# A two-layer graph kernel: batch 0's norm factor put on the adjacency, its halves in two PSUM banks, the mask's operations issued singly, and the second group's second pair normed in the result tiles

## The chip, the core and the metric

The kernel runs on one core of a Trainium2 chip. Five engines work side by side, each through its own list of instructions in order: TensorE (PE, matrix products into PSUM), VectorE (DVE), ScalarE (ACT), GpSimd (POOL) and SyncE (SP, which here issues every DMA). PSUM has eight banks of 128 x 512 float32, named b0 to b7 below. The metric is the device time in microseconds; lower is better.

## What is computed

128 graphs ("batches") of 128 nodes with 512 features, one adjacency for all. Cut to what matters:

```python
def _layernorm(x, axis=-1, eps=1e-5):
    m = jnp.mean(x, axis=axis, keepdims=True)
    v = jnp.var(x, axis=axis, keepdims=True)
    return (x - m) / jnp.sqrt(v + eps)

# layer 0
h = jnp.maximum(_layernorm(x), 0.0)
y = jnp.einsum('nm,bmd->bnd', adj, h)
x = x + jnp.einsum('bnd,do->bno', y, weight) + bias
# layer 1: 8 heads of 64; attn_mask is adj
h = jnp.maximum(_layernorm(x), 0.0)
q, k, v = split(h @ w_qkv)
attn = softmax(where(adj == 0, -inf, q @ k.T * scale))
o = (attn @ v) @ w_proj + b_proj
x = x + o + _layernorm(o) * ln_gamma + ln_beta
```

## The kernel before

The program first collects operations in a list, then a planner orders them, and only then are they issued. `Plan.op` (line 68) takes the engine, an assumed duration, the buffers read and written, and either a due time (`due`) or, for PE, a place (`at`). `schedule` (line 102) walks through time and gives each free engine the ready operation with the smallest due; `early` forbids a start before that time, `urgent` keeps the engine free for an operation that is about to be ready. A buffer is a name out of a group (the table `G`, line 255): it takes a slot such as t20 when its first operation is placed and gives it back after its last. So a changed due or slot can move instructions far from the edit. The planner's times are assumptions of the program; what the chip runs is the resulting order on each engine, with semaphores between them.

**First phase (layer 0).** `phase1` (line 481), one batch at a time for batches 0 to 3, in pairs afterwards. A batch's x is loaded (`load`, line 308); `stats` gives mean and 1/sigma (on DVE for batches 0 to 5: bn_stats and bn_aggr on L393 and L394, then `ve`, POOL's `pow`, and `shift` = -mean/sigma on L404); ACT writes h0 = relu(x/sigma + shift) (L491); four PE matmuls (`mix`, L499) make y = (adj h0) transposed in one PSUM bank, with the transposed adjacency `adjT`; y is copied out. For batches 0 to 3 four float32 matmuls (L508) multiply y with the raw weight tiles `raw0`, which lie in f0 to f3. Later batches split y into three parts (L445 to L447) and do twelve faster fp32r matmuls (L457) against `wA`, the weight split in the same way by `split_weights` (L353 to L357). DVE adds the product to x (L510, or L465 and L470), and the sum is stored twice, as x1d and, with beta added, as x1b.

**The filler.** PE starts with 5 matmuls of the identity on itself (L323), transposes the adjacency (L326), and does 12 more (L332, three operations of four). Their results are not used.

**The mask.** `mask_ops` (line 337) makes from the adjacency an additive mask `maskb`, in six DVE instructions (L339 to L344) that are one operation of the plan, assumed at 1.4, not before 60.

**Second phase (layer 1).** 32 groups of four batches, `phase2_group` (line 571). `fetch` (line 539) brings a pair: x1d is loaded into `xn` (t20, t21), normed with ACT (L555) into `hx` (t22, t23, two slots for all pairs), sent through DRAM and back for a block transpose, transposed on DVE (L559), and split into three parts `hp` by ACT (L562, L565) and POOL (L563, L566). `hp` holds six batches, so batches 6 and 7 write where 0 and 1 were. A group then does q and k (L594, 96 matmuls), the attention products of the group before (L721), scores (L649), v and the projection of the group before (both L457). The second pair of a group is due 8 before the group's start `t0`, 12 for the group with j = 1:

```python
        for p in range(2):
            fetch(group[2 * p:2 * p + 2], t0 - (37, 8 if j != 1 else 12)[p])
```

Slots t18 and t19 are the group "o", in which the projection's results are summed and normed (`sum_up`, L465 and L468). The first of them are written while the second group is computed.

The last groups end with unsplit products and their own norm; no edit touches them.

Of the kernel before, what the change touches and what calls it, by code (L numbers as in the profile page):

```python
# [11 lines left out]
AF = mybir.ActivationFunctionType  # L12
# [3 lines left out]
P = 128  # L16
# [197 lines left out]
def kernel(  # L214
# [77 lines left out]
    def time1(i):  # L292
        return START1 + 4.3 * min(i, FIRST) + T1 * max(i - FIRST, 0)
# [31 lines left out]
    op("PE", 2.2, lambda: idle(5), r=[ident], w=[pa], at=-20)  # L325
# [8 lines left out]
    for _ in range(3):  # L334
        op("PE", 0.9, lambda: idle2(4), r=[ident], w=[pb], at=0)

    def mask_ops():
        e = adj_sb.ap[:, :P]
        nc.vector.tensor_scalar(e, e, 0.0, None, op0=ALU.not_equal)  # L339
        nc.vector.tensor_reduce(some.ap[:, :1], e, AX.X, ALU.max)  # L340
        nc.vector.reciprocal(some.ap[:, :1], some.ap[:, :1])
        nc.vector.tensor_scalar(some.ap[:, :1], some.ap[:, :1], 0.0, None, op0=ALU.mult)
        nc.vector.tensor_scalar(e, e, 1.0, MASKED, op0=ALU.subtract, op1=ALU.mult)
        nc.vector.tensor_scalar(maskb.ap, e, some.ap[:, :1], None, op0=ALU.add)  # L344

    op("DVE", 1.4, mask_ops, r=[adj_sb], w=[adj_sb, some, maskb], due=100, early=60)
# [134 lines left out]
    def phase1(batches):  # L481
        for i in batches:
            if i not in X:
# [3 lines left out]
                       early=6.2 if batches == [1] else 0.0)  # L487
        for n, i in enumerate(batches):
# [12 lines left out]
            if i < FIRST:  # L501
                y = buf("y", [P, C, P])
                op("ACT", 0.53, lambda y=y, p=p: nc.scalar.copy(y.ap, p.ap), r=[p], w=[y], what="y")
# [16 lines left out]
            dma(lambda i=i: X1B[i].ap, lambda i=i: X[i].ap, 256, due=ti + 12, r=[X[i]], w=[X1B[i]], what="x1b out")  # L520

# [17 lines left out]
    def fetch(pair, due):  # L539
# [31 lines left out]
    def phase2_group(j):  # L571
        group = tuple(range(4 * j, 4 * j + 4))
        t0 = START2 + T4 * j
# [5 lines left out]
        for p in range(2):  # L579
            fetch(group[2 * p:2 * p + 2], t0 - (37, 8 if j != 1 else 12)[p])  # L580
# [43 lines left out]
        for n, i in enumerate(group):  # L624
# [3 lines left out]
            op("ACT", 0.53, lambda v=v, a=a: nc.scalar.activation(v.ap, a.ap, AF.Copy, scale=UP), r=[a], w=[v], due=tv + 1, what="vA")  # L628
# [132 lines left out]
    for i in range(FIRST):  # L761
        phase1([i])
# [56 lines left out]
```

## Time and profile before

| | us |
|---|---|
| runs (three) | 2130.49, 2132.52, 2132.86 |
| median | 2132.52 |
| the profiled execution, its own time | 2131.4 |
| its span, first to last instruction | 2129.6 |
| PE busy within the span | 2114.8 |
| first phase's first product with `wA` (L457) begins | 27.79 |
| q and k of the first group (L594) begin | 478.2 |
| q and k of the second group begin | 517.49 |
| PE's last matmul ends | 2121.6 |

The profile gives the instructions of one execution by engine. "PE b L457" is a matmul of line 457 into a PSUM bank; a float32 matmul stands in it as two records, an fp32r matmul as one, so the counts of L323, L332, L499 and L508 are twice the instructions. Where an engine idled, the profile names the instruction that ended the wait. Lines are those of the program before; the edits move them by some tens in the program after.

### The profile page before, as it was taken

The numbers are of one execution on the slowest core, as the hardware profiler recorded it, in microseconds if no ns is written. First come the engines' busy times: TensorE is split into PE (matmuls) and PEld (weight loads), VectorE is DVE, ScalarE is ACT, GpSimd is POOL, SyncE is SP. The second block draws the span as 40 slices with busy tenths as digits, with TensorE's granted clock in tenths as the row PEclk, the third lists the DMA queues.
The fourth block names the chain that finished last, engine by engine and source line by source line (L and its number), as shares of the span: only waits on it lengthen the run. The fifth ranks groups of instructions, "written<-read, shape, count | busy, mean of one in ns | idle before, by whom it ended". The sixth has DMA issues, their size and how long they took to land.

```text
span 2129.6 us, 44884 instructions
## 1 busy us (share of the span) xinstructions
PE 2114.8 (99%) x14867; PEld 1778.1 (83%) x14867; DVE 1729.3 (81%) x3275; ACT 1478.5 (69%) x4240; POOL 1524.9 (72%) x1280
## 2 busy tenths in 40 slices
PE   9999999999999999999999999999999999999998
PEld 7888888887888888888888888888888888888885
DVE  7889888877788778888888887877777788887877
ACT  7777777777666666666666666666666666666664
POOL 6888878794567777776667777777777767677765
PEclk9999999999999999999999999999999999999999
DMA  6676666674655565565556655666666666655553
GB/s 229 222 238 233 229 223 215 232 238 159 189 191 182 182 184 183 180 188 179 179 179 185 195 189 185 190 193 190 186 188 187 188 187 194 192 183 183 182 164 120
DMA packets 297880, 410.96 MB, mean 193 GB/s; under 512 B 33072, under 2 KB 163248, under 8 KB 297648
## 3 DMA queue, kind: packets, MB, share of 16 engines
q1 hardware_dynamic: 297648, 408.09, 60.7%
q8 instruction: 118, 1.93, 0.4%
q14 instruction: 114, 0.93, 0.1%
HBM read 207.68 MB, written 200.28 MB: 192 GB/s over the span
## 4 chain that ended last, share of the span: by engine, by line
PE 94%; DVE 2%; DMA 2%; ACT 1%; issue 1%; SPq 0%; POOL 0%; DVEq 0%; ACTq 0%
PE b L457 47%; PE b L594 32%; PE b L721 5%; PE b L649 5%; PE b L499 5%; DMA t<-in_x_dram 1%; DVE f L659 0%; ACT f L671 0%; DMA f<-in_L_gnn_weight_dram 0%; DMA f<-in_x_dram 0%; DMA d<-t 0%; DVE t L755 0%; DVE wA L357 0%; DVE t L753 0%; DVE t L446 0%
## 5 line engine op out<-in xcount | busy, mean ns | idle before, releaser
L457 PE MATMUL b<-wA,t 128*128 128x512 f32 x2976 | 727.4, 393 | 0.8 <-DVE t L447 0.8
L594 PE MATMUL b<-hp,wqk 128*128 128x512 f32 x3072 | 701.6, 389 | 2.6 <-ACT hp L562 2.6
L594 PEld LDWEIGHTS b<-hp,wqk 128*128 128x128 f32 x3072 | 576.6, 188 | 122.6 <-ACT hp L562 3.0
L457 PEld LDWEIGHTS b<-wA,t 128*128 128x128 f32 x2976 | 549.6, 188 | 109.8 <-DVE t L447 1.2
L671 ACT ACTIVATE f<-f,n 128x128 f32<-128x128 f32 x1024 | 395.8, 389 | 1.3
L747 POOL TENSOR_TENSOR t<-t,t 128x512 f32<-128x512 f32 x128 | 165.9, 1296 | 317.3 <-DVE t L468 247.1
L457 PE MATMUL b<-wv,hp 128*128 128x512 f32 x1536 | 373.0, 392 | 0.6 <-DVE f L659 0.6
L457 PEld LDWEIGHTS b<-wv,hp 128*128 128x128 f32 x1536 | 285.9, 188 | 64.6 <-DVE f L659 6.0
L677 POOL TENSOR_TENSOR f<-f,n 128x1024 f32<-128x1024 f32 x126 | 242.1, 1921 | 65.8 <-PE b L457 42.9
L601 ACT ACTIVATE t<-b 128x512 f32<-128x512 f32 x256 | 148.2, 592 | 199.7 <-PE b L594 199.6
L702 DVE STREAM_TRANSPOSE f<-f 128x1024 f32<-128x1024 f32 x126 | 156.3, 1241 | 130.3 <-DMA f<-d 126.7
L602 DVE TENSOR_TENSOR t<-b,t 128x512 f32<-128x512 f32 x256 | 173.8, 690 | 83.3 <-PE b L594 74.9
L445 ACT ACTIVATE t<-b 128x512 fp32r<-128x512 f32 x248 | 146.6, 592 | 85.0 <-PE b L499 39.8
L446 DVE TENSOR_TENSOR t<-b,t 128x512 fp32r<-128x512 f32 x248 | 170.4, 687 | 38.4 <-ACT t L445 37.0
L671 ACT ACTIVATION_READ_ACCUMULATOR f<-f,n 128x1 f32 x1024 | 193.3, 189 | 0.0
L750 POOL TENSOR_TENSOR t<-t,gamma_b 128x512 f32<-128x512 f32 x122 | 157.7, 1293 | 38.3 <-ACT t L749 38.3
L563 POOL TENSOR_TENSOR hp<-t,hp 128x512 fp32r<-128x512 f32 x128 | 164.6, 1293 | 25.2 <-DMA t<-x1b 14.1
L447 DVE SCALAR_TENSOR_TENSOR t<-t,b 128x512 fp32r<-128x512 f32 x248 | 168.4, 679 | 8.2
L659 DVE TENSOR_TENSOR f<-b,maskb 128x512 f32<-128x512 f32 x256 | 156.6, 682 | 17.4 <-PE b L649 17.4
L566 POOL TENSOR_TENSOR hp<-hp 128x512 fp32r<-128x512 f32 x128 | 165.1, 1300 | 0.2
L555 ACT ACTIVATE t<-t,m 128x512 f32<-128x512 f32 x128 | 97.1, 807 | 91.7 <-DVE m L435 91.7
L751 POOL TENSOR_TENSOR t<-t,t 128x512 f32<-128x512 f32 x122 | 157.4, 1290 | 2.5
(122 smaller groups left out, 3159.8 us busy)
## 6 DMA issues: line engine op xcount, KB each, us to landing
d<-f SPq DMA_DIRECT2D x126, 512.0 KB, 3.5
f<-d SPq DMA_DIRECT2D x504, 128.0 KB, 3.8
t<-x1d SPq DMA_DIRECT2D x128, 256.0 KB, 4.0
d<-t SPq DMA_DIRECT2D x128, 256.0 KB, 4.0
t<-d SPq DMA_DIRECT2D x512, 64.0 KB, 2.3
t<-x1b SPq DMA_DIRECT2D x128, 256.0 KB, 3.0
out_dram<-t SPq DMA_DIRECT2D x128, 256.0 KB, 3.2
t<-in_x_dram SPq DMA_DIRECT2D x91, 256.0 KB, 3.0
```

Source lines behind the costliest of these rows:

```text
L446: op("DVE", 0.63, lambda: nc.vector.tensor_tensor(l.ap, p.ap, h.ap.bitcast(F32), op=ALU.subtract), r=[p, h], w=[l], what=name + "l", due=d ...
L447: op("DVE", 0.63, lambda: nc.vector.scalar_tensor_tensor(s.ap, h.ap.bitcast(F32), UP, p.ap, op0=ALU.mult, op1=ALU.subtract), r=[p, h], w=[ ...
L457: nc.tensor.matmul(p.ap, lhsT=parts[m][2]()[:, c], rhs=w.ap[:, m, c, :], start=start and c == 0, stop=stop and c == C - 1)
L563: op("POOL", 1.35, lambda ht=ht, h=h, l=l: nc.gpsimd.tensor_tensor(l(), ht(), h().bitcast(F32), op=ALU.subtract), r=[h1, HP[i, 0]], w=[HP[ ...
L566: op("POOL", 1.38, lambda l=l, s=s: nc.gpsimd.tensor_tensor(s(), s().bitcast(F32), l().bitcast(F32), op=ALU.subtract), r=[HP[i, 1]], w=[HP ...
L594: nc.tensor.matmul(p.ap, lhsT=wqk.ap[:, which, c, col:col + P], rhs=hp[:, pick, :, which, c, :], start=start and c == 0, stop=stop and c = ...
L602: op("DVE", 0.63, lambda r=r, b=b: nc.vector.tensor_tensor(r.ap, b.ap, r.ap, op=ALU.add), r=[b], w=[r], due=tg + (4 if g < 7 else 2), what ...
L671: nc.scalar.activation(v[:, h], v[:, h], AF.Exp, bias=mx.ap[:, h:h + 1], scale=scale, accum_out=mx.ap[:, H + h:H + h + 1])
L677: op("POOL", 1.93, lambda heads=heads, mx=mx: nc.gpsimd.tensor_tensor(heads().rearrange("p h q r -> p q h r"), heads().rearrange("p h q r ...
L747: op("POOL", 1.32, lambda x1=x1, o=o: nc.gpsimd.tensor_tensor(x1.ap, x1.ap, o.ap, op=ALU.add), r=[o], w=[x1], due=tl + (3 if rank > 1 else ...
L750: op("POOL", 1.32, lambda o=o: nc.gpsimd.tensor_tensor(o.ap, o.ap, gamma_b.ap, op=ALU.mult), r=[gamma_b], w=[o], due=tl + 7, what="gamma")
L751: op("POOL", 1.32, lambda x1=x1, o=o: nc.gpsimd.tensor_tensor(o.ap, o.ap, x1.ap, op=ALU.add), r=[x1], w=[o], due=tl + 9, what="out")
```

## The change

Five edits.

1. Batch 0 gets its own function, `first_batch`. Its x is loaded in two halves of 256 columns, ahead of the adjacency. Each half has its own bn_stats. DVE, no longer ACT, writes h0 = max(x - mean, 0), without the factor 1/sigma; since that factor is positive and belongs to a row of h0, it can stand on the rows of the transposed adjacency, which DVE scales into `adjS` in a free part of the adjacency's tile. Mix, copy and product are done in halves, the two halves of mix in two PSUM banks.
2. The filler is 6 matmuls before the transposition and 3 after it, for 5 and 12.
3. For batches 1 to 3 the product with the raw weight is two operations of two matmuls; the copy of y is urgent. Batch 1's statistics may start at 4.8, for 6.2.
4. The six mask instructions are operations of their own, with starts not before 60, 75, 90, 105, 120 and 135.
5. In the second phase, batches 6 and 7 use the slots of "o" (t18, t19) as `hx`. The second pair is due 20, 20 and 11 before `t0` for the first three groups; all groups but the first have a `t0` smaller by 3; the first group's v copy is due 5 sooner.

```diff
-    load(0, -9)
+    X[0] = buf("x", [P, D])
     adj_sb = buf("raw", [P, D])
-    dma(lambda: adj_sb.ap[:, :P], lambda: adj, 64, due=-8.5, w=[adj_sb], what="adj")
+    dma(lambda: X[0].ap[:, :D // 2], lambda: x[0][:, :D // 2], 128, w=[(X[0], 0)], what="load", due=-60)
+    dma(lambda: X[0].ap[:, D // 2:], lambda: x[0][:, D // 2:], 128, w=[(X[0], 1)], what="load", due=-59)
+    dma(lambda: adj_sb.ap[:, :P], lambda: adj, 64, due=-58, w=[adj_sb], what="adj")
...
-    op("PE", 2.2, lambda: idle(5), r=[ident], w=[pa], at=-20)
+    op("PE", 2.75, lambda: idle(6), r=[ident], w=[pa], at=-20)
...
-    for _ in range(3):
-        op("PE", 0.9, lambda: idle2(4), r=[ident], w=[pb], at=0)
...
-    op("DVE", 1.4, mask_ops, r=[adj_sb], w=[adj_sb, some, maskb], due=100, early=60)
+    op("PE", 1.4, lambda: idle2(3), r=[ident, pa], w=[pb], at=0)
...
-                       early=6.2 if batches == [1] else 0.0)
+                       early=4.8 if batches == [1] else 0.0)
...
-                def plain(a=a, y=y):
-                    for c in range(C):
-                        nc.tensor.matmul(a.ap, lhsT=y.ap[:, c], rhs=raw0[c].ap, start=c == 0, stop=c == C - 1)
-                op("PE", 3.43, plain, r=[y] + raw0, w=[a], at=ti, what="l0")
+                for k in range(2):
+                    def plain(k=k, a=a, y=y):
+                        for c in (2 * k, 2 * k + 1):
+                            nc.tensor.matmul(a.ap, lhsT=y.ap[:, c], rhs=raw0[c].ap, start=c == 0, stop=c == C - 1)
+                    op("PE", 1.72, plain, r=[y] + raw0[2 * k:2 * k + 2], w=[a], at=ti + 0.1 * k, what="l0")
...
+    def first_batch():
+
+        half = lambda b, k: b.ap[:, k * (D // 2):(k + 1) * (D // 2)]
+        h0, t, ends = buf("h0", [P, D]), buf("st1", [P, 16]), buf("st1", [P, 16])
+        for k in range(2):
+            op("DVE", 0.42, lambda k=k: nc.vector.bn_stats(ends.ap[:, 6 * k:6 * k + 6], half(X[0], k)), r=[(X[0], k)], w=[(ends, k)], what="bn")
+        op("DVE", 0.2, lambda: nc.vector.bn_aggr(t.ap[:, 12:14], ends.ap[:, :12]), r=[ends], w=[(t, 0)], what="bn")
+        op("DVE", 0.17, lambda: nc.vector.tensor_scalar(t.ap[:, 6:7], t.ap[:, 13:14], EPS, None, op0=ALU.add), r=[(t, 0)], w=[(t, "ve")], what="ve")
+        op("POOL", 0.71, lambda: nc.gpsimd.tensor_tensor(t.ap[:, 8:9], t.ap[:, 6:7], minus_half.ap[:, :1], op=ALU.pow), r=[(t, "ve"), minus_half], w=[(t, "rs")], what="pow")
+        adjS = View(adj_sb, lambda ap: ap[:, P:2 * P])
+        op("DVE", 0.45, lambda: nc.vector.tensor_scalar(h0.ap, X[0].ap, t.ap[:, 12:13], 0.0, op0=ALU.subtract, op1=ALU.max), r=[X[0], (t, 0)], w=[h0], due=-20, what="relu0")
+        op("DVE", 0.2, lambda: nc.vector.tensor_scalar(adjS(), adjT.ap, t.ap[:, 8:9], None, op0=ALU.mult), r=[adjT, (t, "rs")], w=[(adj_sb, "s")], due=-20, what="adjS")
+        p, y, a = [buf("ps", [P, 2, P]) for _ in range(2)], buf("y", [P, C, P]), buf("ps", [P, D])
+        for k in range(2):
+            def mix(k=k):
+                for c in (2 * k, 2 * k + 1):
+                    nc.tensor.matmul(p[k].ap[:, c - 2 * k, :], lhsT=h0.ap[:, c * P:(c + 1) * P], rhs=adjS(), start=True, stop=True)
+            MIX[0] = op("PE", 0.45, mix, r=[h0, (adj_sb, "s")], w=[p[k]], at=-10 + k, what="mix")
+            op("ACT", 0.35, lambda k=k: nc.scalar.copy(y.ap[:, 2 * k:2 * k + 2, :], p[k].ap), r=[p[k]], w=[(y, k)], due=-18 + k, what="y", urgent=True)
...
+            op("PE", 1.72, plain, r=[(y, k)] + raw0[2 * k:2 * k + 2], w=[a], at=time1(0) + 0.1 * k, what="l0")
...
-            HX.append(buf("hx", [P, Q, C, R]))
+            HX.append(buf("o" if 6 <= i < 8 else "hx", [P, Q, C, R]))
...
-        t0 = START2 + T4 * j
+        t0 = START2 + T4 * j - (3.0 if j else 0.0)
...
-            fetch(group[2 * p:2 * p + 2], t0 - (37, 8 if j != 1 else 12)[p])
+            fetch(group[2 * p:2 * p + 2], t0 - (37, (20, 20, 11)[j] if j < 3 else 8)[p])
...
+        (0.26, lambda: nc.vector.tensor_scalar(edges(), edges(), 0.0, None, op0=ALU.not_equal)),
+        (0.29, lambda: nc.vector.tensor_reduce(one(), edges(), AX.X, ALU.max)),
+        (0.16, lambda: nc.vector.reciprocal(one(), one())),
+        (0.15, lambda: nc.vector.tensor_scalar(one(), one(), 0.0, None, op0=ALU.mult)),
+        (0.8, lambda: nc.vector.tensor_scalar(edges(), edges(), 1.0, MASKED, op0=ALU.subtract, op1=ALU.mult)),
+        (1.2, lambda: nc.vector.tensor_scalar(maskb.ap, edges(), one(), None, op0=ALU.add)),
+    )):
+        op("DVE", us, f, r=[adj_sb], w=[adj_sb, some, maskb], due=300, early=60 + 15.0 * k, what="edges")
```

The times in the code are the planner's assumptions, not measurements.

More of the change, by code (lines that the diff above doesn't have):

```diff
@@ L332, in idle2 @@
             nc.tensor.matmul(pb.ap, lhsT=ident.ap, rhs=ident.ap, start=True, stop=True)
-    for _ in range(3):
-        op("PE", 0.9, lambda: idle2(4), r=[ident], w=[pb], at=0)
[L337 to L344, printed above, removed]
-    op("DVE", 1.4, mask_ops, r=[adj_sb], w=[adj_sb, some, maskb], due=100, early=60)
+    op("PE", 1.4, lambda: idle2(3), r=[ident, pa], w=[pb], at=0)
     def split_weights(w, c, col, raw, low, due, gap, early=0.0):
@@ L502, in phase1 @@
                 y = buf("y", [P, C, P])
-                op("ACT", 0.53, lambda y=y, p=p: nc.scalar.copy(y.ap, p.ap), r=[p], w=[y], what="y")
+                op("ACT", 0.53, lambda y=y, p=p: nc.scalar.copy(y.ap, p.ap), r=[p], w=[y], what="y", urgent=True)
                 a = buf("ps", [P, D])
-                def plain(a=a, y=y):
-                    for c in range(C):
-                        nc.tensor.matmul(a.ap, lhsT=y.ap[:, c], rhs=raw0[c].ap, start=c == 0, stop=c == C - 1)
-                op("PE", 3.43, plain, r=[y] + raw0, w=[a], at=ti, what="l0")
+                for k in range(2):
[3 more added lines that the diff above has]
+                    op("PE", 1.72, plain, r=[y] + raw0[2 * k:2 * k + 2], w=[a], at=ti + 0.1 * k, what="l0")
                 op("DVE", 0.68, lambda i=i, a=a: nc.vector.scalar_tensor_tensor(X[i].ap, a.ap, 1.0, X[i].ap, op0=ALU.mult, op1=ALU.add, accum_out=mean(i)),
@@ L520, in phase1, with plain @@
             dma(lambda i=i: X1B[i].ap, lambda i=i: X[i].ap, 256, due=ti + 12, r=[X[i]], w=[X1B[i]], what="x1b out")
+    def first_batch():
[16 more added lines that the diff above has]
+            op("ACT", 0.35, lambda k=k: nc.scalar.copy(y.ap[:, 2 * k:2 * k + 2, :], p[k].ap), r=[p[k]], w=[(y, k)], due=-18 + k, what="y", urgent=True)
+            def plain(k=k):
+                for c in (2 * k, 2 * k + 1):
+                    nc.tensor.matmul(a.ap, lhsT=y.ap[:, c], rhs=raw0[c].ap, start=c == 0, stop=c == C - 1)
+            op("PE", 1.72, plain, r=[(y, k)] + raw0[2 * k:2 * k + 2], w=[a], at=time1(0) + 0.1 * k, what="l0")
+        op("POOL", 1.32, lambda: nc.gpsimd.tensor_tensor(X[0].ap, X[0].ap, b0_b.ap, op=ALU.add), r=[b0_b], w=[X[0]], due=time1(0) + 1, what="b0")
+        finish1(0, a)
@@ new lines, in finish1 @@
+    def finish1(i, a):
+        ti = time1(i)
+        op("DVE", 0.68, lambda: nc.vector.scalar_tensor_tensor(X[i].ap, a.ap, 1.0, X[i].ap, op0=ALU.mult, op1=ALU.add, accum_out=mean(i)),
+           r=[a], w=[X[i], (means, i)], due=ti + 5, what="x1")
+        X1D[i] = in_dram([P, D], "x1d")
+        dma(lambda: X1D[i].ap, lambda: X[i].ap, 256, due=ti + 6, r=[X[i]], w=[X1D[i]], what="x1 out")
+        X1B[i] = in_dram([P, D], "x1b")
+        op("POOL", 1.32, lambda: nc.gpsimd.tensor_tensor(X[i].ap, X[i].ap, beta_b.ap, op=ALU.add), r=[beta_b], w=[X[i]], due=ti + 10, what="beta")
+        dma(lambda: X1B[i].ap, lambda: X[i].ap, 256, due=ti + 12, r=[X[i]], w=[X1B[i]], what="x1b out")
@@ L627, in phase2_group @@
             a, b = times_weights([(HP[i, m], None, part(i, m)) for m in range(3)], wv, tv, "v", [v])
-            op("ACT", 0.53, lambda v=v, a=a: nc.scalar.activation(v.ap, a.ap, AF.Copy, scale=UP), r=[a], w=[v], due=tv + 1, what="vA")
+            op("ACT", 0.53, lambda v=v, a=a: nc.scalar.activation(v.ap, a.ap, AF.Copy, scale=UP), r=[a], w=[v], due=tv + (1 if j else -4), what="vA")
             op("DVE", 0.63, lambda v=v, b=b: nc.vector.tensor_tensor(v.ap, b.ap, v.ap, op=ALU.add), r=[b], w=[v], due=tv + 2, what="vB")
@@ L759, in rest_of @@
         return PT, finish
-    for i in range(FIRST):
+    first_batch()
+    edges = View(adj_sb, lambda ap: ap[:, :P])
+    one = lambda: some.ap[:, :1]
+    for k, (us, f) in enumerate((
+        (0.26, lambda: nc.vector.tensor_scalar(edges(), edges(), 0.0, None, op0=ALU.not_equal)),
[6 more added lines that the diff above has]
+        op("DVE", us, f, r=[adj_sb], w=[adj_sb, some, maskb], due=300, early=60 + 15.0 * k, what="edges")
+    for i in range(1, FIRST):
         phase1([i])
```

## The prediction

> **What bounds the kernel now.** I read the page's busy shares, then who kept TensorE (PE) waiting in the whole span, then the chain of waits of the first 60 us, then rows around each wait. From the page:
>
> ```profile
> PE 2114.8 (99%) x14867; PEld 1778.1 (83%) x14867; DVE 1729.3 (81%) x3275; ACT 1478.5 (69%) x4240; POOL 1524.9 (72%) x1280
> ```
>
> PE is the bound from end to end; only time in which it idles or does filler can be won. The list of its waits (total, times, longest, us) is short:
>
> ```profile
> PE b L594 <- ACT hp L562: 2.6, 1, 2.6
> PE b L323 <- POOL t masks.py:199: 1.4, 1, 1.4
> PE b L499 <- ACT t L491: 1.0, 2, 0.6
> PE b L457 <- DVE t L447: 0.8, 1, 0.8
> PE b L457 <- DVE f L659: 0.6, 1, 0.6
> PE b L649 <- DVE t L447: 0.4, 1, 0.4
> ```
>
> In the timeline they stand at 514.9 (2.57), 0 (1.36), 13.5 (0.40) and 38.0 (0.58), 67.4 (0.81), 2079.3 (0.63) and 545.3 (0.38). Two more stretches carry no work: the filler matmuls (L323, L332), up to 8.07, and the tail after PE's last matmul, 2121.6 to 2129.6. The instruction lists of the two programs are the same on every engine from the third group's first products on (some 590 us), so the tail and the 0.63 stay. What is at stake: the first 28 us, 0.58, 0.81, 2.57 and 0.38.
>
> **The start.** The chain of waits (start, length, what), pieces left out:
>
> ```profile
> 2.11 5.37 DMA f<-in_L_gnn_weight_dram
> 7.50 6.86 DMA t<-in_x_dram
> ...
> 14.38 0.71 DVE m L393
> ...
> 26.16 1.08 DVE wA L357
> ```
>
> It does not pass through batch 0's norm, mix or product. SP's twelfth DMA (x of batch 4) is issued only when the first weight tile has landed (7.48), lands at 14.36, and then VectorE (DVE) is busy without a break: statistics of batches 4 and 5, the splitting of the weight (L354, L357), updates L510. The split weight wA is whole at 27.23, and
>
> ```profile
> 27.79 3.01 PE L457 MATMUL b<-wA,t 128*128 128x512 f32 x12
> ```
>
> is the first product that needs it, of three-part products it does for the rest of the phase.
>
> *The front half.* By rows: x0 landed at 4.06; as two 128 KB DMAs issued at 0.74 and 1.18 I put it at 3.6 (estimate). Two half statistics (0.69 for a whole, so some 0.4 each), 0.18, then max(x-m,0) on DVE (not in the trace; between 0.33, half of L447's 0.67 for such a tile, and ACT's 0.81 that it replaces; I take 0.5), then, by the list, batch 1's statistics (0.87), which wait for x1 (landing 5.0), then the scaled adjacency (128x128: L339's 0.22). That is ready at 6.2. POOL's pow (0.56) lies beside; the two half copies on ACT (0.59 for a whole, between 0.27 and 0.4 each) end before the weights land. Mix starts at 6.3 for 8.07 now, while 9 instead of 17 fillers end at 5.4. The first product's half then waits for the second weight tile (SP's next issue puts it at 8.15; 8.4 with one more DMA issue, 0.43, ahead; between 8.15 and 8.6): 8.4 for 9.85 now. If nothing else stood there, that is the gain: **1.4**.
>
> But the DVE list from x4 on holds the same operations as now (the two-batch and update operations in another order), so the 12.85 us from 14.38 to 27.23 stay. x4's DMA still waits for the first weight tile, which I put 0.1 later: 14.45 + 12.85 = 27.3. And the order is worse for batch 3: its shift (L404) now stands behind batch 4's statistics, the update of batch 0 and batch 5's statistics: 14.45 + 0.87 + 0.68 + 0.87 = 16.9, ACT's relu 0.81, mix 3 at 18.0, where PE is ready at 8.4 + 1.7 + 0.9 + 3.4 + 0.9 + 1.7 = 17.0. It idles 1.0. From there l0 3.43, mix 0.9, l0 3.43, mix 0.85 and 0.9: the first L457 four at 27.5. Its second four need L446, which the list puts behind the update of batch 3: 27.3 + 0.6 + 0.1 + 0.65 + 0.1 = 28.75; now they start at 27.79 + 0.91 = 28.7. **So the start gains 0** (between -0.6, if DVE loses what contention it now escapes, and the full 1.4).
>
> [...] Two stretches of 1 us (length, then busy time and starts of PE, weight loads, DVE, ACT, POOL, then clock, DMA share, GB/s):
>
> ```profile
> 6.00:7.00 1.00, 1.00 (x6) 1.00 (x6) 0.93 (x4) 0.81 (x1) 0.00 (x0) 1.00 1.02 381
> 7.00:8.00 1.00, 1.00 (x11) 1.00 (x10) 0.27 (x2) 0.03 (x1) 0.55 (x1) 1.00 1.05 404
> ```
>
> Half-matmuls begin at 6 or 7 a us until 7.0, then 11: the release came at 7.0, 5.6 us after PE began, though the clock column says 1.00 throughout. In the new program PE is busy to 5.4, idle to 6.3, busy to 8.0: some 80% of the stretch before 7.0. By the row it is released there and the first product costs 1.72 a half; [...] I take the row: 0.
>
> **0.58 at 38.0.** Four x loads into f0 to f3 (SP, from 28.17) stand behind a weight load that waits for L357 (27.23); ACT waits for the first until 33.4. In the new list two of them stand ahead of that load and of x1's store of batch 3, behind x1b of batch 1: freed by PE and the split at about 26, 2 us earlier. I take 0.55 (0.2 to 0.58).
>
> **0.81 at 67.4.** The mask's six operations run as one block:
>
> ```profile
> L343 DVE TENSOR_SCALAR t<-t x1: 848/848/848, 63.4 to 63.4; 128x128 f32<-128x128 f32 x1
> ...
> L344 DVE TENSOR_SCALAR maskb<-t,some x1: 1194/1194/1194, 64.3 to 64.3; 128x128 f32<-128x128 f32 x1
> ```
>
> With 0.22, 0.29, 0.17 and 0.15 they are 2.87, of which 0.81 reached PE: 2.06 of cover. Spread over 75 us or more, none is over 1.2. The block is still done before the first use (503). Gain 0.81 (at least 0.4, if the cover is less elsewhere).
>
> **2.57 at 514.9.** Batches 6 and 7's path, new pieces of the timeline:
>
> ```profile
> 513.62 0.67 DVE L559 STREAM_TRANSPOSE t<-t 128x512 f32<-128x512 f32 x1
> ...
> 516.82 0.61 ACT L562 ACTIVATE hp<-t 128x512 fp32r<-128x512 f32 x1
> ...
> 517.49 22.07 PE L594 MATMUL b<-hp,wqk 128*128 128x512 f32 x96 [2.56 <-ACT hp L562]
> ```
>
> Their two h tiles use t22/t23, which batches 4 and 5 hold until POOL's last part; so their loads go out at 502 to 511 (2 stores, 8 loads on SP), the transposes stand behind eight mask additions (4.88) and three or four maxima, L562 behind two batches' exponentials. Normed in t18/t19 instead, free until the first results, which come after the first attention products (539 to 543), with the pair's due 8 us sooner (12 to 20), the relu, both exchanges, transposes and L562 of batch 6 stand ahead of the masks in the new lists. Batch 7's parts may only overwrite batch 1's after its v product (506 to 509): L562, then POOL 1.3 + 1.3 end by 512. All ahead of 514.9. On SP the pair's twelve DMAs now stand in one row behind the last x1 stores, ahead of the next pair's; on POOL the four operations (5.1) now lie before the first division (513.8), and two of them no longer between divisions, so the exchanges behind those come earlier too. Next late is the fourth transposed tile (L702, ends 541.2, needed at 539.49 + 3 x 0.91 = 542.2 now): with the division before it some 3 us sooner it keeps pace. Gain 2.57 (at least 1.5, if a part of 7 is late). PE's new lists at this point have the parts in plain order, as in later groups, which show no wait; so I also take 0.3 of the 0.38 at 545.3 (0 to 0.38). v's earlier due and the later groups' 3 us change orders only.
>
> **Sum:** 0 + 0.55 + 0.81 + 2.57 + 0.3 = 4.2. The profiled execution was 2131.4 (span 2129.6 and 1.8 around it): 2127.2. The runs shown have a median of 2132.52, 1.1 above; 2128.3 by that. I say **2127.9**, its own range 2126.8 to 2129.0. A difference under 0.2% (4.3 us) can't be told from no change here: 2128.25 is the border, inside that range.
>
> **Rivals.**
> - The front's 1.4 arrives (x4 lands sooner, or DVE runs the split in its short form: L354 took 0.68 to 1.5). For it: PE starts useful work 1.4 sooner. Against: the chain. 2126.5. Chance 0.18.
> - The 2.57 stays in good part: POOL or batch 7's overwriting is the new wait, or the plan's place for it isn't met. 0 + 0.55 + 0.81 + 0.6 = 2: 2130.2. For it: v product and overwriting lie 3 us apart. Chance 0.19.
> - The clock stays at half[...]. Chance 0.13.
> - Slower: group 0's second pair is due 12 us sooner, in the first phase's end, where POOL is busy 67.3 of 78 us and PE never waits (400 to 478). Its work (POOL 5.2, ACT some 5.4) delays the last mixes' y parts; with over 8.5 us of that on PE the sum turns and passes the border: 2137. It decides from the point where PE falls under 0.9 in that stretch. Against: the lists put that pair little earlier there than now. Chance 0.04.
>
> Likeliest: 0.46. Faster takes 0.30 of it, nearly all of the first rival, a little of the others: 0.53; slower 0.04; same 0.43. The range 2125.8 to 2130.6 takes in both neighbours.
>
> **What would show it.** After: first L457 between 27.2 and 28.2 with an idle of about 1 before the fourth mix (front) - right; an L457 at 26.4 - the front arrived. Six to seven half-matmuls a us after 8.4: the clock. No wait at 38, none near 67, L594 following L457 at about 511 without a gap. Wrong if a wait over 1 stands anywhere else in PE's list.

## The result, and the profile after

Seven runs of the changed kernel gave a median of **2126.23 us** (2124.87 to 2126.56), beside 2132.52 (2130.14 to 2133.73) for seven of the kernel before: ratio 0.9974, 95% interval 0.9964 to 0.9984. The whole interval of the gain lies between 3.4 and 7.7 us. The profiled execution was 2126.23 with a span of 2124.4, against 2131.4 and 2129.6.

PE is still the bound, busy for 2111.8 of 2124.4; its busy time fell by 3.0, its idle time by 2.2. The medians are 6.3 apart, the profiled executions 5.2. First the line of busy times, then the whole list of what PE waited for in the changed kernel (total, times, longest, us). Lines have moved: L457 is L447 now, L594 is L622, L649 is L677, L721 is L749, L499 is L489 (L529 for batch 0), L508 is L499 (L535 for batch 0), L491 is L481, L562 is L590.

```profile
PE 2111.8 (99%) x14851; PEld 1775.8 (84%) x14851; DVE 1725.1 (81%) x3277; ACT 1475.5 (69%) x4240; POOL 1522.4 (72%) x1280
```

```profile
PE b L489 <- ACT t L481: 1.7, 2, 1.1
PE b L325 <- POOL t masks.py:199: 1.4, 1, 1.4
PE b L529 <- DVE m L387: 0.7, 1, 0.7
PE b L447 <- DVE f L687: 0.6, 1, 0.6
```

The waits that the prediction counted as won (2.57, 0.81, 0.58 and 0.38) are all gone. The 1.4 before the filler and the 0.6 at the end remain, as expected, and two waits for ACT (0.64 at mix 2, where the kernel before had 0.40, and 1.08 at mix 3) and one for DVE in the first 19 us are the new order's. In the timeline (start, length, engine, line, operation, shape, count; idle before it in brackets) the changed kernel's second group has no bracket left:

```profile
504.04 9.40 PE L447 MATMUL b<-wv,hp 128*128 128x512 f32 x40
513.28 21.92 PE L622 MATMUL b<-hp,wqk 128*128 128x512 f32 x96
535.14 3.71 PE L749 MATMUL b<-f,t 128*64 128x128 f32 x64
538.78 3.72 PE L677 MATMUL b<-t,t 64*64 64x128 f32 x128
```

The start stands in the chain of waits of the changed kernel:

```profile
6.63 8.51 DMA t<-in_x_dram
...
15.16 0.70 DVE t L383
...
17.66 0.82 ACT t L481
18.53 1.16 PE b L489 x8
...
28.34 0.93 PE b L447 x4
```

The chain is the one that the prediction named: batch 4's x, DVE, batch 3's shift and relu, mix 3 after an idle of 1.08, then PE alone up to the first product with `wA`. In this view a piece starts where the one before it ends; the timeline has that product at 28.09, 0.30 later than before (27.79).

**Where the time came from.** An idle that is listed wasn't all of a stall here: around the 0.81 at the mask twelve matmuls took 2.39 and 1.21, where the changed kernel's twelve (at 64.69) take 2.98, and the shortest gaps are not listed. So I compare marks, the starts of the same operation in both traces. Mixes are counted from 0. Those of the first phase stand 3.63 apart where nothing holds PE.

| stretch, from start to start | before | after | gained |
|---|---|---|---|
| to mix 5 | 26.98 | 27.29 | -0.31 |
| mix 5 to mix 10 (the wait at 38) | 19.05 | 18.46 | 0.59 |
| mix 15 to mix 16 (the mask) | 5.06 | 3.63 | 1.43 |
| mix 16 to the first group's v | 436.30 | 436.53 | -0.23 |
| the first group's v to the second group's q and k (the listed wait of 2.56) | 11.97 | 9.24 | 2.73 |
| the second group's q and k themselves | 22.00 | 21.86 | 0.14 |
| the second group's scores | 4.69 | 3.65 | 1.04 |
| from its v to the fourth group's q and k | 72.93 | 72.95 | -0.02 |
| sum: start of the fourth group's q and k | 620.75 | 615.38 | 5.37 |

Mix 10 to 15 takes 18.13 in both, and the attention products between q, k and scores 3.64. From the fourth group on the lead stays (5.34 at PE's last matmul). At two rows the list of waits tells much less than the marks. These are the kernel before's, at the mask, at the first group's v and at the scores:

```profile
64.16 1.05 PE L499 MATMUL b<-t,t 128*128 128x128 f32 x8
64.97 2.39 PE L457 MATMUL b<-wA,t 128*128 128x512 f32 x8
68.17 1.21 PE L457 MATMUL b<-wA,t 128*128 128x512 f32 x4 [0.81 <-DVE t L447]
69.22 1.05 PE L499 MATMUL b<-t,t 128*128 128x128 f32 x8
...
505.52 9.40 PE L457 MATMUL b<-wv,hp 128*128 128x512 f32 x40
...
543.13 2.18 PE L649 MATMUL b<-t,t 64*64 64x128 f32 x66
545.68 2.20 PE L649 MATMUL b<-t,t 64*64 64x128 f32 x62 [0.38 <-DVE t L447]
547.82 1.43 PE L457 MATMUL b<-wv,hp 128*128 128x512 f32 x5
```

From mix to mix it is 5.06, not 3.63: 1.43 lost, of which the bracket shows 0.81. From the first scores matmul to the first of v it is 4.69 where the changed kernel takes 3.65 (538.78 to 542.43): 1.04 lost, the bracket shows 0.38.

### The profile page after: what moved, and what is told of

Read it like the earlier page. It is cut to its first block, busy times and chain, and to the rows that moved or that the text cites. A ratio compares the mean times of both kernels' runs of the same rounds, so it can differ in the third digit from the quotient of the medians.

```text
span 2124.4 us, 44861 instructions
## 1 busy us (share of the span) xinstructions
PE 2111.8 (99%) x14851; PEld 1775.8 (84%) x14851; DVE 1725.1 (81%) x3277; ACT 1475.5 (69%) x4240; POOL 1522.4 (72%) x1280
## 3 DMA queue, kind: packets, MB, share of 16 engines
q8 instruction: 118, 1.93, 0.4%
## 4 chain that ended last, share of the span: by engine, by line
PE 98%; DVE 1%; DMA 0%; SPq 0%; issue 0%; POOL 0%; ACT 0%; DVEq 0%
PE b L447 49%; PE b L622 33%; PE b L749 5%; PE b L677 5%; PE b L489 5%; DMA t<-in_x_dram 0%; PE b L499 0%; SPq L282 0%; DVE t L783 0%; DVE t L781 0%; PE b L768 0%; DVE t L770 0%; DVE m L383 0%; DVE f L687 0%; POOL t L775 0%
## 5 line engine op out<-in xcount | busy, mean ns | idle before, releaser
L447 PE MATMUL b<-wA,t 128*128 128x512 f32 x2976 | 728.5, 393 | 0.0
L622 PE MATMUL b<-hp,wqk 128*128 128x512 f32 x3072 | 702.0, 389 | 0.0
L622 PEld LDWEIGHTS b<-hp,wqk 128*128 128x128 f32 x3072 | 576.7, 188 | 119.7
L447 PEld LDWEIGHTS b<-wA,t 128*128 128x128 f32 x2976 | 549.8, 188 | 108.6 <-DVE t L436 0.9
L447 PE MATMUL b<-wv,hp 128*128 128x512 f32 x1536 | 373.9, 392 | 0.6 <-DVE f L687 0.6
L447 PEld LDWEIGHTS b<-wv,hp 128*128 128x128 f32 x1536 | 285.9, 188 | 64.6 <-DVE f L687 6.2
L630 DVE TENSOR_TENSOR t<-b,t 128x512 f32<-128x512 f32 x256 | 174.0, 690 | 78.4 <-PE b L622 65.5
L594 POOL TENSOR_TENSOR hp<-hp 128x512 fp32r<-128x512 f32 x128 | 165.1, 1300 | 7.1 <-ACT hp L593 4.0
```

The costliest lines, as they stand in the source:

```text
L447: nc.tensor.matmul(p.ap, lhsT=parts[m][2]()[:, c], rhs=w.ap[:, m, c, :], start=start and c == 0, stop=stop and c == C - 1)
L594: op("POOL", 1.38, lambda l=l, s=s: nc.gpsimd.tensor_tensor(s(), s().bitcast(F32), l().bitcast(F32), op=ALU.subtract), r=[HP[i, 1]], w=[HP ...
L622: nc.tensor.matmul(p.ap, lhsT=wqk.ap[:, which, c, col:col + P], rhs=hp[:, pick, :, which, c, :], start=start and c == 0, stop=stop and c = ...
L630: op("DVE", 0.63, lambda r=r, b=b: nc.vector.tensor_tensor(r.ap, b.ap, r.ap, op=ALU.add), r=[b], w=[r], due=tg + (4 if g < 7 else 2), what ...
```

## The experiments

Each kernel is the changed one with the edit shown. Medians and lowest to highest time are given; the ratio is to the kernel before, run beside it on the same chip, with medians of 2131.1 to 2131.7. The profiled execution is one of these runs, and its span is some 1.8 less than its time. My theory: edit 5 brings 2.6 or a little more, the mask 0.8 to 1.4, the wait at 38 some 0.6, and the front nothing, because batch 4's x and DVE's chain set the start. The rival: the front's 1.4 is part of the gain.

### The front undone

Batch 0 again in `phase1` with x in one load, fillers of 5 and 12, one product operation for each batch.

```diff
-    first_batch()
-    for i in range(1, FIRST):
+    for i in range(FIRST):
         phase1([i])
```

> The changed kernel with batch 0 computed as before (one load, whole statistics, ACT's relu, one bank, fillers 5 and 12); mask and second phase as changed. Theory (VectorE's chain from x of batch 4 sets the start; the front costs 0.3 by the mix marks): mix of batch 5 at 26.9 to 27.1, where the changed kernel has 27.29, span 2124.4 less 0.3 plus at most the 0.58 wait at 38, so 2124.1 to 2124.7, the same time as the changed kernel within 0.5. Rival (the front brings 1.4): mix of batch 5 no earlier than 28.0 and a span of 2125.8 or more.

Measured: 2125.97 (2125.07 to 2126.71), ratio 0.9972 (0.9962 to 0.9982). Mix 5 begins at 26.61, and the wait at 38 is back (38.05 is 4.17 after the mix before it, 0.54 more than 3.63). In this execution batch 4's x had landed at 13.53, against 15.14 in the changed kernel's; at mix 10 and at the fourth group it is 0.33 and 0.32 ahead of that one. So the front brings the relief at 38, and by time nothing that can be measured. The theory holds for the time; mix 5 came 0.3 sooner than it said.

### The mask in one block

```diff
+    op("DVE", 1.4, mask_ops, r=[adj_sb], w=[adj_sb, some, maskb], due=100, early=60)
```

> The changed kernel with the six mask operations again as one block of the plan. Theory (the block cost 1.43, from mark to mark, of which the list of waits shows 0.81): one stretch from mix to mix near 60 to 70 is longer than 3.63 by 1.2 to 1.5 and the span is 2125.6 to 2125.9. Rival (the list is right): longer by 0.8, span 2125.2. Second rival (other order there, cover enough): no long stretch, span 2124.4.

Measured: 2127.65 (2126.27 to 2129.24), ratio 0.9981 (0.9973 to 0.9989). By the medians the block costs 1.4; the intervals of the two ratios overlap. In its timeline:

```profile
62.75 1.05 PE L489 MATMUL b<-t,t 128*128 128x128 f32 x8
63.56 1.17 PE L447 MATMUL b<-wA,t 128*128 128x512 f32 x4
65.07 1.20 PE L447 MATMUL b<-wA,t 128*128 128x512 f32 x4 [0.34 <-DVE t L436]
66.10 1.05 PE L489 MATMUL b<-t,t 128*128 128x128 f32 x8
```

The next mix follows at 70.67: 7.92 for two spacings of 3.63, so 0.66 lost at the block, not 1.43. In this order the block ended at 63.8 (65.5 in the kernel before) and met other work. None of the three expectations was met: span 2125.8 as the theory said, but not with its stall.

This run is 1.13 ahead of the changed kernel at mix 10 (its x of batch 4 landed at 13.70) and 1.49 behind at the fourth group, so it lost 2.6 between. Besides the block there are three stretches of 0.68 (161 to 169), 0.65 (249 to 253) and 0.37 (307 to 315) and 0.22 in the second group's scores, none with a wait in the list. Three of the four runs below that have the split sooner lose 0.7 near 105 in the same way with the mask spread, so such losses come without the block; whether these three belong to it stays open. That spreading the mask helps is likely; its size is 0.66 at its place and 1.4 by the medians, and not settled further.

### The second group's pair as before

All of edit 5 undone: the tiles, the due times, the 3 us and v's copy.

```diff
-            HX.append(buf("o" if 6 <= i < 8 else "hx", [P, Q, C, R]))
+            HX.append(buf("hx", [P, Q, C, R]))
...
-        t0 = START2 + T4 * j - (3.0 if j else 0.0)
+        t0 = START2 + T4 * j
...
-            fetch(group[2 * p:2 * p + 2], t0 - (37, (20, 20, 11)[j] if j < 3 else 8)[p])
+            fetch(group[2 * p:2 * p + 2], t0 - (37, 8 if j != 1 else 12)[p])
...
```

> The changed kernel without the edits of the second phase (old slots, dues, group start). Theory: the wait of 2.6 for L562 before the second group's q and k is back, and with it the hole in that group's scores, 1.0 from mark to mark though listed as 0.4: span 2124.4 + 2.57 + 1.04 + 0.15 = 2128.2. Rival (only the listed waits count): 2127.3. Rival (the 2.57 came from the front's order, not from these edits): 2124.4 to 2125.

Measured: 2130.09 (2128.94 to 2132.54), ratio 0.9994 (0.9986 to 1.0003): most of the whole change's gain is gone, 3.2 by the mark of the fourth group (618.58). In its timeline the wait is back to the hundredth, the hole in the scores is not:

```profile
516.23 22.06 PE L622 MATMUL b<-hp,wqk 128*128 128x512 f32 x96 [2.56 <-ACT hp L590]
...
541.86 3.85 PE L677 MATMUL b<-t,t 64*64 64x128 f32 x128
```

The scores take 3.78 to the next matmul of v, 0.13 above the changed kernel's 3.65. So the 1.04 there isn't edit 5's: 0.9 of it stay won without it. It comes with the shifted lists, and which edit freed it stays open. The span, 2127.5, is near the 2127.3 of the rival that counts only the listed waits, and short of the theory's 2128.2 for want of that hole.

### Edit 5 in two parts: old tiles, then old due times

Old tiles with the new due times:

```diff
-            HX.append(buf("o" if 6 <= i < 8 else "hx", [P, Q, C, R]))
+            HX.append(buf("hx", [P, Q, C, R]))
```

> Edit 5 with its due times but without the result tiles: batches 6 and 7 are normed in the third kind of tile again. Theory (the tile sets the start of the path: it is free only when batches 4 and 5 have been taken out of it, some 502 us): the loads can't go out sooner however early they are due, so at least the 2.6 us at the second group's q,k come back, and whatever is queued behind these loads on SP waits with them: 2128.5 to 2133, with the wait of PE for ACT (line of L590) of 2.5 or more in the list. Rival (the due times alone put the relu, the exchanges and the transposes ahead of the masks): no wait there, 2126 as the changed kernel.

Measured: 2132.37 (2131.40 to 2134.41), ratio 1.0006 (0.9997 to 1.0015), by the medians 2.3 slower than without any of edit 5 (the intervals overlap). The list of PE's waits:

```profile
PE b L622 <- ACT t L629: 2.1, 1, 2.1
PE b L622 <- ACT hp L590: 1.4, 2, 1.2
...
PE b L677 <- DVE t L437: 0.8, 1, 0.8
```

No wait stands before the second group's q and k, which begin at 512.78. The 2.1 stands in the middle of them (525.95), for ACT's copy out of PSUM, the 0.8 in that group's scores, and of the 1.4 there are 1.2 before the fourth group's q and k (621.45) and 0.2 at 2001. Up to 512 ACT is short of work (busy 6.1 of the 12 us from 500 on, in the changed kernel 8.1), from there it is busy without a break, and it comes to that copy at 525.33, in the changed kernel at 522.71. So the loss comes, as the theory said, but not as a late start of the path: the wait of 2.5 for L590 was not there. What fits, and wasn't tested further: with early due times the work that needs the tiles stands ahead of other work on ACT, and that other work is late.

New tiles with the old due times: `t0`, the pair's due and v's copy as in the diff above and the part on edit 5 in the change.

> Edit 5 with the result tiles but with all due times of before (pairs, groups 3 us later, v's first half). Theory (two things are needed, the free tile and the place ahead of the mask additions in DVE's list): the loads go out early, but the transposes stay behind the masks, so most of the 2.6 us at the second group's q,k is back: 2128.5 to 2130 if the rest of the order stays. More is possible, since without the 3 us of earlier due the later groups' parts may meet the result tiles' new users: up to 2145, then with a repeated wait of 0.3 to 0.6 a group. Rival (the free tile is all of it): no wait at 513, 2126.

Measured: 2141.90 (2136.47 to 2143.24), ratio 1.0049 (1.0034 to 1.0064), four runs. From the list of PE's waits, and two stretches (length, then busy time and starts of PE, weight loads, DVE, ACT, POOL, then clock, DMA share, GB/s):

```profile
PE b L622 <- ACT hp L590: 6.0, 8, 2.0
...
513.39:516.81 3.42, 1.37 (x7) 0.82 (x6) 1.35 (x3) 3.42 (x16) 2.98 (x2) 1.00 0.38 153
516.81:520.22 3.41, 3.41 (x10) 2.65 (x9) 0.43 (x2) 3.38 (x16) 2.39 (x3) 0.50 0.63 186
```

2.05 of the 6.0 are back before the second group (515.94), and sixteen of the later groups come 51.2 to 52.9 us apart instead of 51.05. The wait costs more than itself here: after it the clock is at half for 3.41 us, and the group's q and k take 23.60, 1.74 more than in the changed kernel. So both halves are needed for the gain: neither the free tiles nor the due times brought any of it alone. That the 3 us of lead are what keeps the later groups' h parts in time was not tested apart from the other due times.

### The split of the weight sooner

The first weight's split may start 3 us sooner; statistics of batches 4 and 5 not before 15.

```diff
-                       early=4.8 if batches == [1] else 0.0)
+                       early=4.8 if batches == [1] else 15.0 if batches == [4, 5] else 0.0)
-..., time1(FIRST) - 7 + 1.5 * c, 0.5, 12.0 + 1.5 * c)
+..., time1(FIRST) - 7 + 1.5 * c, 0.5, 9.0 + 1.5 * c)
```

> The changed kernel with the split of the first weight allowed 3 us sooner in the plan (9, 10.5, 12, 13.5 for 12, 13.5, 15, 16.5) and the statistics of batches 4 and 5 not before 15 in the plan, so that batch 3's shift and part of the split stand ahead of them on VectorE. Theory (the chain from x of batch 4 through the split bounds the start): the split weight is whole by 26.5 or sooner (27.95 in the changed kernel), mix of batch 3 waits 0.3 or less for 1.08, and the span falls by 0.8 to 1.7: 2122.7 to 2123.6. Rival (the DMA of x of batch 4 or contention with POOL sets it, whatever the order): span 2124.0 to 2124.8.

Measured: 2125.58 (2124.61 to 2126.75), ratio 0.9971 (0.9960 to 0.9983): not told apart from the changed kernel. Mix 3 waited for nothing, and `wA` was whole at 24.5, 3.4 sooner than in the changed kernel, but PE came to it only at 27.59. In this execution mix 0 took 2.08 for eight matmuls and the first product 2.90 for four, where the changed kernel's first execution has 1.16 and 1.98: half clock. The span of 2125.0 misses both the theory's (2122.7 to 2123.6) and the rival's. So the next question was the clock.

### When the clock is released

The changed kernel once more, as it is:

> The changed kernel once more, as it is, for a second look at when the clock is released and for its time on the same chip. Theory (with 9 fillers, ended before mix 0, it depends on the execution whether the clock is released by 6.4 or only at some 10): mix 0's eight matmuls take either 1.1 to 1.2 us or 2.0 to 2.1 us, and the time is 2125.5 to 2126.5 in either case, since batch 4's x and VectorE's chain come no sooner. Rival (release by 6.4 is this kernel's rule): 1.1 to 1.2 us.

Measured: 2125.89 (2124.42 to 2126.57), ratio 0.9971 (0.9960 to 0.9982). In the timeline, first the changed kernel's first profile, then this second one:

```profile
6.44 1.16 PE L529 MATMUL b<-t,t 128*128 128x128 f32 x8 [0.73 <-DVE m L387]
7.62 1.98 PE L535 MATMUL b<-f,t 128*128 128x512 f32 x4
```

```profile
7.02 2.08 PE L529 MATMUL b<-t,t 128*128 128x128 f32 x8 [1.16 <-DVE m L387]
8.89 2.55 PE L535 MATMUL b<-f,t 128*128 128x512 f32 x4
```

The same instructions take 1.16 or 2.08. I read the two as full and half clock; for the one slow stretch within the work (new tiles, old due times) the clock record has 0.50. Seven executions were profiled with these 9 fillers: the changed kernel twice, the mask in one block, edit 5 undone, its two halves, the split sooner. Three were at full clock at mix 0 (the changed kernel's first and both halves of edit 5); four were so only from some 10 us on. Yet the first product with `wA` began at 28.09 in the changed kernel's first execution and at 27.85 in the second, because batch 4's x had landed at 15.14 and here at 14.88: DVE's chain covers the half clock.

The clock column of the stretches says 1.00 in both; the record that it reads holds no entry before the release and is then taken as full. The first entry stands at 5.53 in the changed kernel and at 10.23 here (7.05 in the kernel before).

Nearly no filler at all, one before the transposition:

```diff
-    op("PE", 2.75, lambda: idle(6), r=[ident], w=[pa], at=-20)
+    op("PE", 0.45, lambda: idle(1), r=[ident], w=[pa], at=-20)
-    op("PE", 1.4, lambda: idle2(3), r=[ident, pa], w=[pb], at=0)
```

> The changed kernel with one filler matmul pair before the transposition of the adjacency and none behind it (fillers compute nothing that is used); all other lists as they are. Theory (the clock is released after a long enough busy stretch, and what the fillers add is only an earlier start of it): PE is busy from the mix of batch 0 on (6.4), so the eight mix matmuls take 2.06 us and the first products stay at half clock to some 10 to 13; the first three-part product (L447 here, shifted by the edit) starts at 27.5 to 29.5, time 2126 to 2128. Rival (fillers decide nothing, VectorE's chain alone sets the start): 2126.0 plus or minus 0.5, first three-part product at 27.5 as in the three runs in which the clock stayed at half to about 10.

Measured: 2126.54 (2125.87 to 2127.09), ratio 0.9978 (0.9971 to 0.9985). Half clock for mix 0 (2.07) and the first product (2.73 for four), full from mix 1 (10.50) on; first product with `wA` at 27.51. That is the rival's number for the start, and 0.04 above its range for the time: without fillers nothing is lost that can be measured.

Five fillers behind the transposition, so that PE has no gap before mix 0:

```diff
-    op("PE", 1.4, lambda: idle2(3), r=[ident, pa], w=[pb], at=0)
+    op("PE", 1.4, lambda: idle2(5), r=[ident, pa], w=[pb], at=0)
```

> The changed kernel with five fillers instead of three behind the transposition (they compute nothing that is used), so that PE has no gap from 1.36 to the first product. All other lists as they are. Theory (a busy stretch without the gap of 0.3 to 0.8 us before mix 0 releases the clock by some 8 us in each execution, as with the 17 fillers of before): mix 0's eight matmuls take 1.2 to 2.1 us, mix 1 starts at 9.4 to 10.0 instead of 10.9 to 11.1. But VectorE's chain from x of batch 4 on stays, so the time stays at 2126 plus or minus 0.7. Rival (the half clock at the start is what costs the front's 1.4): 2124.7 to 2125.2.

Measured: 2125.95 (2125.55 to 2128.02), ratio 0.9979 (0.9971 to 0.9987). In its timeline:

```profile
6.54 1.10 PE L529 MATMUL b<-t,t 128*128 128x128 f32 x8
...
26.48 4.25 PE L447 MATMUL b<-wA,t 128*128 128x512 f32 x16
```

Here the front's full 1.3 arrives (26.48 against 27.79 before): the clock is released and batch 4's x landed early, at 13.53. The kernel with the front undone had the same landing and began it at 27.42. The second group's q and k begin at 511.75, 1.53 sooner than in the changed kernel. But the fourth group's begin at 614.93, only 0.45 sooner. The time is the theory's, for a reason that it didn't have. The other 1.1 is lost in the second group's scores:

```profile
537.24 3.38 PE L677 MATMUL b<-t,t 64*64 64x128 f32 x113
541.39 0.66 PE L677 MATMUL b<-t,t 64*64 64x128 f32 x15 [0.78 <-issue]
```

"issue" means that the trace shows nothing that PE waited for. The split sooner has this hole too, behind matmul 117 (0.23 listed, 0.65 by the marks).

### Both at once, and the hole in the scores

Split sooner and five fillers:

> The run with the split allowed 3 us sooner, with five fillers instead of three behind the transposition (they compute nothing that is used). In that run the split weight was whole at 24.5 but PE, at half clock to about 10, came to it only at 27.8; in the run with five fillers alone PE came at 26.5 but the start was worth 1.5 us at the second group and 0.5 at the end. Theory (the start is held by two things at once, the clock and VectorE's chain, and each must go): the first three-part product starts at 25.7 to 26.3, the second group's q,k at 511.0 to 511.8. A hole of 0.7 in the second group's scores stays, as in both of those runs, and takes part of it back: 2124.3 to 2125.5. Rival (what is won at the start is all given back by the second group's scores): 2125.6 to 2126.4.

Measured: 2125.57 (2125.29 to 2125.92), ratio 0.9973 (0.9962 to 0.9983). Mix 0 took 1.16 at 6.33, `wA` was whole at 24.7, but mix 2 waited 0.93 for ACT, and the first product with `wA` began at 26.98, not by 26.3. The second group's q and k began at 511.91, and the hole stood again behind scores matmul 113, with 0.47 listed. The fourth group's began at 614.81. Between theory and rival; most of what was won is given back.

The hole stood behind matmul 113 in both programs with 22 filler records, behind 117 in the run with 18 (split sooner): four records sooner for four more in front. So it is a place in the program, behind matmul record 3112 from its start in all three, and not a moment. The next edits change only the count. All fillers in two of 64 columns, 11 matmuls or 22 records more:

```diff
-            nc.tensor.matmul(pa.ap, lhsT=ident.ap, rhs=ident.ap, start=True, stop=True)
+            nc.tensor.matmul(pa.ap[:64, :64], lhsT=ident.ap[:, :64], rhs=ident.ap[:, :64], start=True, stop=True)
...
-    op("PE", 2.75, lambda: idle(6), r=[ident], w=[pa], at=-20)
+    op("PE", 2.75, lambda: idle(12), r=[ident], w=[pa], at=-20)
...
```

> The run before (split sooner, five fillers) with each filler matmul (they compute nothing that is used) in two of 64 columns: 22 matmuls in the program more in front of everything else (in the records, where a filler of 128 columns stands twice, 22 records more), nothing else changed. Open is what the unlabelled hole in the second group's scores is; it stood behind scores matmul 113 in the two runs with 22 filler records and behind 117 in the one with 18. Theory (PE waits there for the next block of its instructions, which the DMA queue named instruction in the trace brings; the block's border lies a fixed number of PE instructions from the program's start): the hole moves to 22 matmuls sooner, behind scores matmul 91, and is again 0.4 to 0.9. Rival (an operand or a bank is late there): the hole stays behind matmul 113. Time by both 2125 to 2126.5.

Measured: **2124.86** (2124.60 to 2125.16), ratio 0.9968 (0.9957 to 0.9980), the fastest median of all. Neither happened: in its timeline the scores have no hole.

```profile
26.45 3.94 PE L447 MATMUL b<-wA,t 128*128 128x512 f32 x16
...
537.53 3.73 PE L677 MATMUL b<-t,t 64*64 64x128 f32 x128
```

The view of the DMA queues has a queue q8 named "instruction", with packets of 16 KB. In the run before this, the packet of that stretch began to move at 539.05, here at 536.57. In the changed kernel, without a hole, it began at 539.43, but PE came to that place only at 542.0. So a smaller step, only the five fillers behind the transposition in halves (10 records more):

> The run with the split sooner and five fillers, with only those five fillers (they compute nothing that is used) in two of 64 columns: 10 matmul records more in front, where the run before this one had 22 more and no hole at all, its block of instructions having come at 536.4 to 536.8, ahead of the burst of loads, where it had come at 538.8 to 539.2 with the hole. Theory (the hole is PE's wait for the block; the border moves with the count, and the wait goes when the block is fetched ahead of the burst): if the block still comes in the burst, the hole stands behind scores matmul 103; if not, there is none. Rival (an operand or a bank): a hole behind matmul 113. Time 2124.6 to 2125.8.

Measured: 2125.68 (2124.93 to 2126.91), ratio 0.9976 (0.9965 to 0.9986); the packet began at 536.62, no hole, and the scores took 3.65. That fits the instruction block and speaks against a late operand, which 10 filler records could hardly hasten. The two packets did not move ahead of the burst of loads, as the expectation has it: the queues moved 414 and 422 GB/s in the half microsecond from 536.5 on.

All packets of q8 in the fourteen traces say more. There are 118 in each, for 30,192 to 30,276 records of PE's list, so one for each 256, and packet k never begins before PE has begun 148 records beyond 256k (packets and records counted from 0). In all three runs with the hole it stands at record 256k + 449 with k = 23, so I count the time from a packet's end to PE's arrival there, for every k:

| run | PE begins record 256k + 148 | packet begins | ends | PE goes on | without its hole (estimate) |
|---|---|---|---|---|---|
| five fillers | 535.18 | 538.96 | 539.93 | 541.39 | 0.51 after the end |
| split sooner, five fillers | 535.35 | 539.05 | 540.01 | 541.27 | 0.60 |
| split sooner | 536.81 | 539.98 | 540.87 | 542.48 | 1.20 |

At the other 1,635 places in the traces PE arrives 1.47 or more after the packet's end, and none has such a wait in the list (at 1.53, in the mask in one block, the scores are 0.22 longer without one). The three packets had begun 3.2 to 3.8 after record 256k + 148; at k = 23 in the other eleven traces it is 1.1 to 2.9. So in these traces PE stops where, and only where, it comes to such a place within 1.2 us of the end of the block's packet. This leaves the block as the cause, with one reserve: the place of the border is read from the holes themselves, and no run moved the hole to a third place.

## Why the prediction was right

The kernel got faster, and the whole interval of the ratio lies below 1. The forecast of 2127.9 was 1.7 above the median of 2126.23. Of that, 0.7 is the choice to stand between the profiled execution and the median of three (the sum from the profiled one gave 2127.2), and 1.0 is in the terms. The median lies below the likeliest case's own range (2126.8 to 2129.0) and nearer to the first rival's 2126.5 than to the forecast; only the traces tell that the rival's reason was not at work. By the marks the terms' 4.2 became 5.4, with errors both ways:

- **Start, predicted 0, measured -0.3 at mix 5.** The mechanism was right to the wait: an idle of 1.0 before mix 3, measured 1.08 at 18.53 (predicted 18.0). DVE's chain took 12.8 from batch 4's x to the whole `wA` (predicted 12.85). What was late is the landing, 15.14 for 14.45. In eight executions with the changed front and the split as it was, x landed between 13.53 and 15.14, and in seven of them the first product with `wA` began 12.95 to 13.02 later, at half clock or full. So the -0.3 is one execution's landing. The prediction had one fixed landing for it. The contention of DVE that its range allows for stands in the kernel before: of the eight operations on L354 and L357 the five with 0.47 or more of their time beside a 128x512 operation of POOL took 1.02 to 1.75, the three with 0.26 or less 0.68.
- **The clock.** I took the trace's row of the kernel before (released 5.6 us after PE's start) as the measure for the new program, and that did not hold for each execution: of the seven with 9 fillers, three were at full clock at mix 0. The one stretch of half clock within the work (new tiles, old due times) is 3.413 us long in the trace's clock record, and the stretches of full clock are whole multiples of that (621 in the kernel before, 619 in the changed kernel, 618 in its second execution). In the 3.41 us that ended with the release PE was busy for 0.90 to 1.00 in the fourteen traces; in those that ended without one, for 0.89 at most. With 9 fillers PE was busy from 1.36 to between 5.4 and 6.2; what decides from one execution to the next whether the release comes by mix 0 was not shown. The prediction's stretch before 7.0, counted as 3.41, is by its own times 0.74 busy and not 0.8; neither would have been enough in these traces. In all six kernels with more fillers (17, 11, or the halves) the clock was full at mix 0. The half clock cost nothing where the idle before mix 3 covers it: the changed kernel's first product with `wA` began 12.95 after the landing at full clock and 12.97 after it at half. In the mask in one block, where x landed at 13.70, it was not covered: PE had no idle, and the first product came 13.56 after the landing, 0.6 more than in the others.
- **0.55 at 38.** Measured 0.59 at the marks from mix 5 to mix 10; with the front undone the wait is back (0.54), and 0.35 of the stretch. That it is the order of the x loads was not tested by itself.
- **0.81 for the mask.** The changed kernel gained 1.43 there; the term was the bracket, not the stall. The block put back cost 0.66 at its place and 1.4 in the medians.
- **2.57 at the second group.** Right: gone, 2.73 by the marks, and back with 2.56 when edit 5 is undone. The q and k begin at 513.28. The sign that the prediction gave, 511, does not follow from its own terms: 517.49 less 0.55, 0.81 and 2.57 is 513.56. The next guard named (the fourth transposed tile) kept pace. Both halves of the edit are needed, as the prediction had it (free tiles and a place ahead of the masks); that either alone would do harm it did not say.
- **0.3 of 0.38 in the scores.** Measured 1.04; again the bracket for the stall. The reason that I gave, edit 5's lists, holds for 0.1 at most: 0.9 stayed won without them. The gain here is luck.

The 0.23 that the changed kernel lost between mix 16 and the first group's v was in no term.

Of the rivals, the first (the front's 1.4 arrives) did not happen in the changed kernel, but did in one execution with two fillers more and an early landing, and was then given back 500 us later. The clock at half did happen, to some 10 us, in four of seven executions; it was covered in two of them (not in the mask in one block, nor with the split sooner, where DVE's chain ends at 24.5). The slower one (group 0's second pair in the busy end of the first phase) did not: PE has no wait there.

## What to carry to other kernels

Size a stall by marks in the trace, the spacing of the same operation with and without it; the idle that the profile lists was 0.81 of 1.43 and 0.38 of 1.04. A step that waits for buffers needs both the free buffer and a place in the queues: either alone brought no gain here, and the free tiles alone a loss of 10 us. When time won early doesn't reach the end, look for the first place where the lead shrinks, and ask whether it is fixed to a moment or to a place in the program.

## What the hardware showed

- The same program starts its first products at full or at half clock from one execution to the next (1.16 or 2.08 for mix 0), and the clock column says 1.00 for both. The matmul's own duration tells it.
- A wait cost the clock once. With the old due times a wait of 2.05 left PE busy for 1.37 of the 3.42 us from 513.39 on, and the clock was at half for the next 3.41. The kernel before had a longer wait at the same work, 2.56, but it lay across two stretches of 3.41, counted from the release at 7.05 (PE busy for 2.70 and 1.56), and the clock stayed at 1.00.
- PE stalled 0.65 to 1.1 us, by the marks, at a place that moved with the count of PE instructions ahead of it. The DMA queue named "instruction" moved 118 packets of 16 KB (1.93 MB) in each trace, one for each 256 records of PE's list, and at 1,635 of 1,638 places PE came 1.47 or more after the packet's end and did not wait like this. In the scores PE works through some 35 matmuls and 35 weight loads a microsecond (128 matmuls in 3.65), so that a packet which begins 3.2 to 3.8 us after its place in the list has been passed comes too late there. The counts of the three holes and the packets of all traces support this cause; what kept the packets back was not tested.
- Batch 4's x, issued between 6.38 and 6.63, landed between 13.3 and 15.1 in the twelve executions with the changed front, which have the same DMAs ahead of it.
